# A decoder layer on one core: attention weights split over two tiles, seven products in another order, half-width first batches, separate PSUM tiles for the last rows

## The chip, the core and the metric

The kernel runs on one NeuronCore of a Trainium2 chip. TensorE multiplies matrices (its weight loads are listed apart, as PEld), VectorE (DVE) and ScalarE (ACT) work on SBUF and PSUM, GpSimd (POOL) on SBUF alone, and SyncE (SP) issues most DMAs. Each engine and each DMA queue takes its instructions in order and waits where an operand is not ready. The metric is the device time in microseconds of one execution, median of several.

## The reference, cut to what matters

The input x has 16 batches of 128 rows by 1024, all float32; the context has the same shape. One pre-norm decoder layer is computed:

```python
x = x + attn(layernorm(x))            # one head, d = 256
x = x + xattn(layernorm(x), context)  # 8 heads of 64, linear attention
x = x + ffn(layernorm(x))             # int4 weights, inner width 2752

# attn
q, k, v = split(x @ Wqkv + bqkv)
out = softmax(q @ k.T / 16) @ v @ Wo + bo
# xattn: Wq, Wk, Wv, Wo; softmax of q over a head's channels, of k over the positions
context = k @ v.T ; out = context.T @ q ; out = Wo @ out + bo ; l2-normalised, times g * sqrt(128)
# ffn: weights unpacked from two nibbles a byte, (w - zero) * scale in groups of 64
out = (silu(x @ Wg.T) * (x @ Wu.T)) @ Wd.T
```

## The kernel before, in words

The layer runs in three stages on one core. Self-attention takes about the first 245 us, cross-attention goes on to about 755, and the feed-forward block takes the rest.

*Self-attention* works on four token tiles of 512 tokens, that is four batches each (`TB`, `BPT`, `NT` in the code). Rows are normalised by ScalarE, turned by TensorE transposes through PSUM, and copied into `xnT`, with the 1024 channels on the partitions in eight chunks. In the first tile the opening (`first_rows`) does this batch by batch; its vector instructions are pinned in program order by `InOrder`, a wrapper that asks the planner to keep their order. Then `query_key` multiplies query and key blocks f = 0 to 3 directly, each in two halves of 256 tokens. In the three later tiles `query_key_products` computes all of query and key by a Strassen-like scheme: seven products of quarter-size operands instead of eight. The operands on the weight side are quarters of the query and key weights and their sums S1, S2, S4 (`weight_sums`); on the data side they are quarters of `xnT` and their sums T1, T2, T3, made by VectorE. Products 1, 6, 5 and 3 add up in one PSUM bank, read by ScalarE or VectorE between them; products 7 and 4 share another; product 2 has its own.

Beside a tile's products stand pieces of other work. `beside(f)` adds the output bias on GpSimd, takes statistics of a coming batch, gives a finished batch of the tile before its output projection (`give`, L330 and L337), and turns a batch of the next tile. `value(i)` multiplies a value block. `next(early)` runs one step of `prepare`, which unpacks the feed-forward weights: SP loads packed bytes (`raw`) and scales (`sz`), VectorE unpacks into `pa` and combines into `pc`, GpSimd stores them to DRAM. These vector steps are pinned among themselves. Where nothing is pinned, a planner orders each engine's instructions by program order and by its own estimates of when operands are ready; it also orders the SP queue.

*Memory.* Pools are stacked from the left and from the right of SBUF. Self-attention's pool `a_w` holds the joint weight tile `wqkv_sb` (24 KB a partition: queries and keys in the first 16, values in the last 8), then the output weights, biases and S1, S2, S4. When self-attention is over, the pools of cross-attention take the same left place (`unit_pool`), in the order `b_ek`, `b_as`, `b_cx`, `b_0`, `b_w`, `b_3`; with `reuse_waits="tile"` a new tile waits for the last users of the old tiles that lie where it comes to lie. So the two context tiles `cx` (`load_ctx`, L790) lie 16 KB up, on the values' part of the joint tile, and `wk_sb`, `wq_sb` (L805, L811) on biases. The context's transpose `cxt` and `wo_again`, a second copy of the output weights for the last four batches, lie on the right.

*Cross-attention* starts with four key units of its first batch (`key_unit`: context chunk by `wk_sb`, then an exponential on ScalarE into `ek`, then a product with `cxt`). From line 692 on TensorE, VectorE and SP instructions are pinned, so whatever stands first in these streams holds up the rest.

*The last product.* The down projection is a scheme of seven outer products with seven inner ones each, in the orders `DOWN` and `INNER`. The last inner product (2) of the last outer one (4) ends the kernel: it adds to the PSUM tile of product 1, four batches wide, first for rows 0 and 1, then for rows 2 and 3; `got` adds the kept sum `U` for each row and sends it out.

## Time and profile before

| What | Value |
|---|---|
| Median of three runs | 2178.35 us (2177.74 to 2178.78) |
| Profiled execution, its own time | 2177.33 us |
| Its span in the profile | 2175.5 us |
| Mean granted TensorE clock | 0.997 |
| TensorE busy | 2147.1 us, 99% of the span |
| Weight loads busy | 1671.9 us, 77% |
| VectorE busy | 1547.0 us, 71% |
| DMA, mean over the span | 218 GB/s |

Durations and stretches are read from the profiled execution; 1.8 us of its time lie outside its span. In a row of the timeline the first number is the start in us from the span's start, the second the length in us, then engine, line, operation, output and inputs, shapes, and the number of instructions taken together; a bracket gives the engine's idle time before it and what ended that. A matmul of float32 appears as two instructions. In the list of waits a row gives who waited for whom, the total in us, how often, and the longest. TensorE instructions of one row overlap in the array, so their number divided into the length gives their spacing, and that is shorter than the duration of one.

### The profile page before, as it was taken

How to read it: one execution, taken by the hardware profiler on the slowest of the kernel's cores; microseconds unless marked ns; L12 is line 12 of the kernel's file. 1: busy time of each engine (PE TensorE's matmuls, PEld its weight loads, DVE VectorE, ACT ScalarE, POOL GpSimd, SP SyncE). 2: the span in 40 equal slices, each digit the busy share in tenths (PEclk: the TensorE clock that was granted, in tenths of full speed). 3: DMA queues.
4: the chain of work that ended last, by engine and by line, in shares of the span. 5: the costliest groups of instructions: out<-in, count | busy, mean ns of one | idle time of the engine just before them, and what ended most of it. 6: DMA issues, size and time to landing. Idle time of an engine off the chain costs nothing.

```text
span 2175.5 us, 26039 instructions
## 1 busy us (share of the span) xinstructions
PE 2147.1 (99%) x9148; PEld 1671.9 (77%) x9148; DVE 1547.0 (71%) x2102; ACT 546.7 (25%) x746; POOL 796.7 (37%) x675
## 2 busy tenths in 40 slices
PE   8999899999999999999999999999999999999998
PEld 7877545555555558888888888888886788888887
DVE  5989678888888758786777987878774445534573
ACT  4121135555655551212111212112111000000000
POOL 5343224333433345544444554444441022333200
PEclk9999999999999999999999999999999999999999
DMA  6445537777787576877888746677667578979941
GB/s 259 131 149 187 187 126 236 226 228 236 236 267 245 184 235 216 291 254 257 268 291 278 241 141 215 205 228 244 207 207 232 186 201 241 282 197 258 269 124 60
DMA packets 272205, 474.59 MB, mean 218 GB/s; under 512 B 29633, under 2 KB 128321, under 8 KB 266177
## 3 DMA queue, kind: packets, MB, share of 16 engines
q1 hardware_dynamic: 226736, 383.02, 54.6%
q0 software_dynamic: 27456, 71.45, 12.1%
q10 hardware_dynamic: 17872, 18.36, 2.6%
q8 instruction: 75, 1.23, 0.2%
q14 instruction: 66, 0.53, 0.1%
HBM read 314.64 MB, written 157.55 MB: 217 GB/s over the span
## 4 chain that ended last, share of the span: by engine, by line
PE 93%; DVE 4%; issue 1%; DMA 1%; ACT 0%; SPq 0%; POOL 0%; DVEq 0%; ACTq 0%; POOLq 0%
PE q L80 38%; PE po L2031 22%; PE kq L80 10%; PE mm L80 8%; PE kx L80 5%; PE p L80 3%; PE mm L451 2%; PE mm L436 1%; DVE pa L80 1%; PE mm L573 1%; PE mm L330 1%; DMA cx<-in_cx 1%; DVE pc L80 0%; PE tr L381 0%; DVE bnst L147 0%
## 5 line engine op out<-in xcount | busy, mean ns | idle before, releaser
L80 PE MATMUL q<-ti,li 128*128 128x256 f32 x1680 | 385.4, 379 | 0.0
L80 PEld LDWEIGHTS q<-ti,li 128*128 128x128 f32 x1680 | 319.2, 190 | 43.4
L80 ACT COPY k<-q 128x512 f32<-128x512 f32 x210 | 123.1, 586 | 661.1 <-PE q L80 642.6
L80 POOL TENSOR_TENSOR li<-w 128x512 f32<-128x512 f32 x140 | 203.3, 1458 | 52.0 <-PE q L80 34.5
L974 POOL TENSOR_TENSOR qe<-qe,qrec 128x1024 f32<-128x1024 f32 x64 | 146.3, 2286 | 175.2 <-DVE qrec L80 156.6
L80 POOL TENSOR_TENSOR li<-w,li 128x512 f32<-128x512 f32 x70 | 107.8, 1541 | 259.4 <-PE q L80 239.4
L2031 PE MATMUL po<-wc,lc 128*128 128x256 f32 x840 | 183.4, 379 | 0.0
L2031 PEld LDWEIGHTS po<-wc,lc 128*128 128x128 f32 x840 | 159.6, 190 | 21.8
L80 DVE TENSOR_TENSOR C<-q,k 128x512 f32<-128x512 f32 x150 | 102.8, 685 | 71.8 <-PE q L80 67.4
L80 PE MATMUL q<-b,w 128*128 128x256 f32 x640 | 151.2, 379 | 0.0
L80 POOL TENSOR_TENSOR li<-li,w 128x512 f32<-128x512 f32 x70 | 91.4, 1306 | 123.1 <-PE q L80 122.8
L80 PEld LDWEIGHTS q<-b,w 128*128 128x128 f32 x640 | 121.6, 190 | 17.0 <-issue 0.5
L80 PE MATMUL q<-ti,w 128*128 128x256 f32 x560 | 132.3, 379 | 0.0
L80 PE MATMUL kq<-wk_sb,cx 128*128 128x512 f32 x256 | 121.9, 599 | 7.8 <-DMA cx<-in_cx 7.8
L80 PEld LDWEIGHTS mm<-qs,m_sb 128*128 128x128 f32 x512 | 97.3, 190 | 40.1 <-issue 29.9
L2031 PE MATMUL po<-wq,lq 128*128 128x256 f32 x560 | 126.8, 379 | 0.8 <-DVE m L80 0.8
L80 PE MATMUL kx<-ek,cxt 128*128 128x512 f32 x256 | 121.7, 598 | 0.0
L80 DVE STREAM_TRANSPOSE kt<-qe 128x1024 f32<-128x1024 f32 x64 | 79.2, 1238 | 58.9 <-POOL qe L974 56.8
L80 PE MATMUL mm<-qs,m_sb 128*128 128x256 f32 x512 | 120.8, 379 | 0.0
L80 PE MATMUL kq<-wq_sb,xn 128*128 128x512 f32 x256 | 120.2, 593 | 0.4 <-ACT qe L962 0.4
L2031 PEld LDWEIGHTS po<-wq,lq 128*128 128x128 f32 x560 | 105.9, 190 | 16.7 <-DVE m L80 1.2
L80 PEld LDWEIGHTS q<-ti,w 128*128 128x128 f32 x560 | 106.4, 190 | 14.5
(220 smaller groups left out, 3751.0 us busy)
## 6 DMA issues: line engine op xcount, KB each, us to landing
ti<-r SPq DMA_DIRECT2D x36, 1024.0 KB, 7.6
w<-wg SPq DMA_DIRECT2D x140, 256.0 KB, 3.2
w<-wu SPq DMA_DIRECT2D x140, 256.0 KB, 3.9
lq<-h SPq DMA_DIRECT2D x140, 256.0 KB, 5.2
kd<-kt SPq DMA_DIRECT2D x62, 512.0 KB, 3.5
qs<-kd SPq DMA_DIRECT2D x244, 128.0 KB, 3.1
h<-h SPq DMA_DIRECT2D x80, 256.0 KB, 3.1
wq<-wd SPq DMA_DIRECT2D x70, 256.0 KB, 7.0
```

What stands on the lines that cost most here:

```text
L80: return lambda *args, **kw: self._tc.keep_in_program_order(fn(*args, **kw))
L330: tensor.matmul(ps, oT[:, d, ts(b % BPT, S)], wo_d[d][:, ts(h, 512)], start=(d == 0), stop=(d == 1),)
L436: nc.tensor.matmul(ps[:, tokens], wqkv_sb[:, f, c, :], xnT[:, c, tokens], start=(c == 0), stop=(c == CC - 1),)
L451: nc.tensor.matmul(ps, xnT[:, c, ts(i, S)], wqkv_sb[:, 4:6, c, :], start=(c == 0), stop=(c == CC - 1),)
L573: nc.tensor.matmul(ps[:, n], L[p][:, n, c], R[p][:, c], start=(p == first and n == c == 0), stop=(p in (2, 3, 4) and c == HC - 1), skip_gr ...
L974: nc.gpsimd.tensor_tensor(qe, qe, rec.unsqueeze(2).to_broadcast(wide), ALU.mult)
L2031: nc.tensor.matmul(bank[:, i, :], l[:, ts(i, S)], w,  start=(start and c == 0 and i % 2 == 0), stop=(stop and c == len(pairs) - 1), skip_g ...
```

## The change

The diff has four parts.

1. The opening. Batches 0 and 1 are normalised in two halves of 512 columns, each in its own tile. `first_rows` becomes a generator: it returns before batches 2 and 3 are turned, and these two are turned after the first and the second query block. The statistics of batches 4 to 7 are pinned on VectorE and stand behind it.
2. The products. TensorE's product matmuls are pinned. Their order goes from 1, 7, 6, 2, 5, 4, 3 to 1, 2, 7, 6, 5, 4, 3, the first value block stands between 5 and 4, and the steps of weight preparation are placed one by one (`steps(n)`). In the last token tile the value block that came before the products now comes after product 6, one `give` stands between 5 and 4, and 5 instead of 8 preparation steps come before product 3 in program order, with one left over after the loop.
3. The memory. A pool `a_q` below `a_w` holds the query and key weights (16 KB) and S1, S2, S4; the value weights get their own tile `wv_sb` in `a_w`. Among cross-attention's pools `b_cx` and `b_w` come first, so that context tiles and `wk_sb`, `wq_sb` lie on the query and key weights; `b_0` comes to lie on the value weights.
4. The end. The last inner product keeps rows 0 and 1 in product 1's PSUM tile and puts rows 2 and 3 into tiles of their own (of products 6 and 5). What product 1 holds for rows 2 and 3 is added to `U` by VectorE earlier, at inner product 5.

```diff
+        tc.tile_pool(name="a_q", bufs=1) as aq,
         tc.tile_pool(name="a_w", bufs=1) as aw,
...
-        wqkv_sb = aw.tile([P, 6, CC, P], F32, name="wqkv_sb")
+        wqk_sb = aq.tile([P, 4, CC, P], F32, name="wqk_sb")
+        wv_sb = aw.tile([P, 2, CC, P], F32, name="wv_sb")
...
+            normed = {}
+
             def rows(b):
-                xn = a2.tile([P, C], F32, name="xn")
                 row_shift(b, vector)
-                normalise_act(xn, X[b], b)
-                halves[b] = turn_half(xn, xnT, b, 0)
-                nc.scalar.copy(*turn_half(xn, xnT, b, 1))
+                xn = normed[b] = [
+                    a2.tile([P, C], F32, name="xn") for _ in range(2 if b < 2 else 1)
+                ]
+                n = C // len(xn)
+                for h, t in enumerate(xn):
+                    normalise_act(t[:, ts(h, n)], X[b][:, ts(h, n)], b)
+
+            def turn_rows(b):
+                halves[b] = turn_half(normed[b][0], xnT, b, 0)
+                nc.scalar.copy(*turn_half(normed[b][-1], xnT, b, 1))
...
-            for b in range(1, BPT):
-                half(b, 0)
-                rows(b - 1)
-                if b > 1:
-                    copy(b - 2)
-                half(b, 1)
-            rows(BPT - 1)
-            copy(BPT - 2)
-            copy(BPT - 1)
+            half(1, 0)
+            rows(0)
+            turn_rows(0)
+            half(1, 1)
+            half(2, 0)
+            rows(1)
+            turn_rows(1)
+            copy(0)
+            half(2, 1)
+            copy(1)
+            half(3, 0)
+            rows(2)
+            half(3, 1)
+            rows(3)
+            yield
+            turn_rows(2)
+            copy(2)
+            yield
+            turn_rows(3)
+            copy(3)
...
-        S1, S2, S4 = (aw.tile([P, 2, HC, P], F32, name=f"S{n}") for n in (1, 2, 4))
+        S1, S2, S4 = (aq.tile([P, 2, HC, P], F32, name=f"S{n}") for n in (1, 2, 4))
...
-                        nc.tensor.matmul(
+                        tensor.matmul(
...
+            if t == 0:
+                for f in range(4):
+                    halves[f] = aps.tile([P, TB], F32, name="mm")
+                    query_key(f, xnT, qkT, halves[f], ts(0, HALF))
+                    next(opening, None)
+                for b in range(BPT, 2 * BPT):
+                    row_stats(b, InOrder(tc, nc.vector))
...
-                for i in (2, 3) if more else ():
-                    value(i, xnT, v)
+                if more:
+                    value(2, xnT, v)
+                    value(3, xnT, v)
                 third()
-                value(0, xnT, v)
-                for f, ps in enumerate(((1, 7), (6, 2), (5, 4), (3,))):
-                    for p in ps:
-                        product(p)
-                    if f < 2 or not more:
-                        beside(f)
-                    elif f == 2:
-                        next(early)
-                value(1, xnT, v)
-                at = weigh(qkT)
+                for p in (1, 2, 7):
+                    product(p)
+                beside(0)
+                steps(3)
+                product(6)
+                beside(1)
+                steps(2)
+                if not more:
+                    value(0, xnT, v)
+                product(5)
                 if more:
+                    value(0, xnT, v)
+                else:
+                    give((t - 1) * BPT, oT)
+                product(4)
+                if more:
+                    steps(1)
+                    product(3)
+                    value(1, xnT, v)
+                    at = weigh(qkT)
                     beside(2)
+                    steps(2)
                     turned = []
                     beside(3, lambda: turned.append(turn_weights(at)))
+                    steps(2)
                     atT = turned.pop()
                 else:
-                    for i in range(1, BPT):
+                    beside(2)
+                    beside(3)
+                    product(3)
+                    value(1, xnT, v)
+                    at = weigh(qkT)
+                    steps(1)
+                    for i in range(2, BPT):
+                        value(i, xnT, v)
                         give((t - 1) * BPT + i - 1, oT)
-                        if i > 1:
-                            value(i, xnT, v)
-                        next(early, None)
+                        steps(2)
...
+    bcx = unit_pool("b_cx", 2)
+    bw = unit_pool("b_w", 1)
     bek = unit_pool("b_ek", 3)
     bas = unit_pool("b_as", 1)
-    bcx = unit_pool("b_cx", 2)
     b0 = unit_pool("b_0", 2)
-    bw = unit_pool("b_w", 1)
...
-                            start=(start and c == 0 and i % 2 == 0),
+                            start=(start and c == 0 and (i % 2 == 0 or len(rows) == 1)),
...
-                    for rows in (range(2), range(2, BPT)):
-                        multiply(ps, pairs, False, True, rows)
-                        got(oq, (0, 0), ps, only=rows)
+                    multiply(ps, pairs, False, True, range(2))
+                    got(oq, (0, 0), ps, only=range(2))
+                    for i, q in ((2, 6), (3, 5)):
+                        own = dps[q].tile(wide, F32, name=f"po{q}")
+                        multiply(own, pairs, True, True, (i,))
+                        got(oq, (0, 0), own, only=(i,))
...
+                    if oq == DOWN[-1]:
+                        apart = U[0, 0][:, 2:]
+                        vector.tensor_tensor(apart, bank[1][:, 2:], apart, ALU.add)
```

## The prediction

> **What bounds the kernel now.** I read the busy table first, then the list of who waited for whom, then the busy time by stage, then the three places where TensorE waits. The busy table:
>
> ```profile
> PE 2147.1 (99%) x9148; PEld 1671.9 (77%) x9148; DVE 1547.0 (71%) x2102; ACT 546.7 (25%) x746; POOL 796.7 (37%) x675
> ```
>
> TensorE is idle for 2175.5 - 2147.1 = 28.4 us of the span, and the change takes away no matmul. So what can be won lies in those 28.4 us and in instructions that run slower than their kind. The waits of TensorE:
>
> ```profile
> PE tr L381 <- ACT xn L164: 8.2, 1, 8.2
> PE kq L80 <- DMA cx<-in_cx: 7.8, 1, 7.8
> PE mm L573 <- DVE qkT L561: 2.7, 2, 1.7
> PE mm L573 <- ACT qkT L555: 0.9, 1, 0.9
> PE po L2031 <- DVE m L80: 0.8, 1, 0.8
> ```
>
> The reader sees one wait for each part of the change: 8.2 at the start, 7.8 at the crossing from self-attention to cross-attention, 2.7 + 0.9 in the seven products, 0.8 at the last tile. By stage (stretch, its length, then busy time of PE, PEld, DVE, ACT, POOL, granted clock, DMA share, GB/s):
>
> ```profile
> 145.00:188.00 43.00, 41.27 (x195) 31.03 (x195) 38.88 (x59) 11.05 (x26) 16.95 (x23) 1.00 0.44 147
> 188.00:245.00 57.00, 56.07 (x246) 43.23 (x244) 56.69 (x91) 6.83 (x20) 21.29 (x37) 1.00 0.63 207
> ...
> 245.00:250.00 5.00, 0.24 (x3) 0.05 (x1) 2.27 (x6) 0.59 (x1) 1.50 (x3) 0.96 1.02 405
> 250.00:253.00 3.00, 0.00 (x0) 0.01 (x1) 0.00 (x0) 0.00 (x0) 0.00 (x0) 0.50 1.05 389
> 253.00:255.00 2.00, 1.98 (x3) 0.97 (x4) 0.00 (x0) 0.00 (x0) 0.00 (x0) 0.50 0.49 127
> ```
>
> From 188 to 245 VectorE is busy 56.69 of 57 us, most of it weight preparation (tiles pa, pc): beside TensorE it is the second bound there, and a term won on TensorE in this stage is only kept where VectorE's part comes in time. From 245.24 to 253.02 TensorE has nothing, the DMA engines are full (405 GB/s), and the granted clock falls to 0.50. The crossing in order of time:
>
> ```profile
> 235.97 3.62 PE L451 MATMUL mm<-wqkv_sb,xnT 128*128 128x256 f32 x16
> ...
> 239.66 0.33 SPq L810 DMA_DIRECT2D wo_again<-in_wo  x1
> ...
> 241.81 0.46 SPq L790 DMA_DIRECT2D cx<-in_cx  x1
> ...
> 253.02 5.35 PE L80 MATMUL kq<-wk_sb,cx 128*128 128x512 f32 x8 [7.78 <-DMA cx<-in_cx]
> ...
> 255.66 0.15 DVE L80 TENSOR_SCALAR gs_sb<-gs_sb 128x1 f32<-128x1 f32 x1 [8.32 <-DMA gs_sb<-in_xg]
> ```
>
> The last value product ends at 239.4, SP starts issuing at 239.66, the context load goes out fifth at 241.81 and lands 11.1 us later. The whole queue of attention loads is 0.25 us behind that last read of the joint weight tile. The start and the end:
>
> ```profile
> 8.20 3.83 PE L381 MATMUL tr<-ident,xn 128*128 128x128 f32 x16 [8.20 <-ACT xn L164]
> ...
> 12.55 2.07 PE L436 MATMUL mm<-xnT,wqkv_sb 128*128 128x256 f32 x4 [0.52 <-DVE xnT L80]
> ...
> 18.53 15.71 PE L436 MATMUL mm<-xnT,wqkv_sb 128*128 128x256 f32 x72
> ```
>
> ```profile
> 2163.73 2.42 PE L2031 MATMUL po<-wq,lq 128*128 128x256 f32 x10 [0.85 <-DVE m L80]
> ...
> 2169.22 0.76 DVE L80 TENSOR_TENSOR m<-po,u 128x256 f32<-128x256 f32 x2 [5.54 <-PE po L2031]
> ```
>
> **Part 1, the opening.** Removed: the order in which TensorE meets the transposes of batches 2 and 3 before query block 0 is done (only 8 of its 16 instructions run before 18.53). Added: two half activations for batches 0 and 1 in place of one. The trace has no such half from SBUF here; the 128x512 activation of qkT takes 0.69, the full one 1.24. So the first transposes start at 6.91 + 0.69 = 7.6 instead of 8.20. Batch 1's first half is ready at 8.77 + 0.69 = 9.46, its four transposes at 0.21 each end at 10.3, its copy on VectorE no longer stands behind a bn_stats (0.68) and a shift (0.16) and runs at 10.5 to 11.2. The query weights are there: the first block was issued at 2.60 and its load takes about 7.8, so 10.4; the other three land at about 11.6, 12.9 and 14.3. Block 0 starts at 11.2 instead of 12.55.
>
> From there stand 64 instructions of the four first halves and 16 transposes without a wait. Before, the first halves ended at 18.53 + 56 x 15.71/72 = 30.75. What I don't know is the rate: before, instructions ran at half rate from 8.20 to about 17.5 (0.427 apart in the row at 12.55, 0.218 in the row at 18.53), for 9.3 us, although the granted clock is listed as 1.00. With half rate until 7.6 + 9.3 = 16.9: 13.3 instructions by then, 50.7 x 0.218 + 16 x 0.11 = 12.8 after, end 29.7, gain 1.0. With full rate from 11.2: end 26.9, gain 3.8. Against this: VectorE's statistics of batches 4 to 7 now stand in order behind the copy of batch 3, which comes after block 1 on TensorE, about 22.8. Copy 0.7, four statistics at 1.45, rstd 0.2, POOL 1.0, shift 0.2 and one activation of 1.25 end at 32; TensorE wants that batch's transposes at 34.24 less the gain. So the cover is about 1 us and vanishes with a larger gain. I take **-1.2**, near the row of half rate, with ends +0.5 (the statistics come later than worked out) and -3.8.
>
> The Trainium skill ("TensorE: Matmul & The Clock Gate", section "Part 1: The HAM clock gate (the "warmup" mystery)") has the array go to full rate after one busy window of some 3.4 us. Counted from 11.2 this would be 14.6, an estimate from that page, with the first halves done at 28.5 and a gain of 2.2; the case's own stretch of 9.3 us with small holes of 0.52 speaks for less, and the sum goes by the row.
>
> **Part 2, the products.** No instruction is added. Products 2 and 7 change places with 6, the first value block goes between 5 and 4, and the preparation steps move. In the second and third token tile product 3 waited 1.02 and 1.73 for the vector add of product 5, because only product 4 (3.45) lay between. Now a value block (3.45) and product 4 lie between, 6.9 us, so both waits go: -2.75. What they need keeps its place: 7 comes 13.8 us after the tile's start before and after, 6 comes 21.6 after it in both, and 4 comes 11.2 after 6 in both. In the last tile the 0.93 wait of 6 for an ACT read goes too, since 2 and 7 now stand between 1 and 6. But there value block 0 no longer comes first: 7 is wanted 6.9 us after the tile's start (188.0), at 194.9, and its operand T3 was written at 196.61 to 197.83, behind preparation steps. Pinned, TensorE can't take another product meanwhile: +2.9. Sum -2.75 - 0.93 + 2.9 = **-0.8**; ends -3.7 (T3 in time) and +3.0 (VectorE, saturated, is later by what TensorE has gained, and nothing of the first two waits is kept). Three of 36 preparation steps move behind the last weighing; VectorE does the same total, and after 247.33 it had 8.3 us free.
>
> **Part 3, the crossing.** Query and key weights get a tile at the bottom of the stack, and the context tiles and wk, wq lie on it. Its last readers are products 4 and 3, over by 216.98 before and by about 219 in the new order, at least 20 us ahead of 241.81. Loads of 256 or 512 KB took 3.3 to 11.2 us here, so even the longest is over. Removed: the wait of 7.78, and the half rate after it (8 instructions in 5.35 against 8 x 0.43 = 3.43: 1.92). Together -9.70. What is late next: the key product needs PSUM banks read by the last vector add (ends 245.71) and ACT copy (245.28 + 0.59 = 245.87), 0.6 behind the last matmul. Further on, left at their old times, cxt (landed 247.2, first used 258.21) allows 11.0 us, wvo (255.2, used 266.88) 11.6, the second context (257.6, used 272.06) 14.4. The closest is VectorE: its in-order stream opens with gs_sb at 255.66, whose load stood behind xbo_sb, which waited until 253.0 for the last stores of prepared weights. From there ones, shift, one X add (0.69) and the key sum (1.21) free the first ek buffer at 257.9, and ACT used it again at 266.99: 9.1 us allowed. Those stores landed in the full stretch; 1 MB less in it (context, wk, wq) is 2.5 us at 405 GB/s, so some 11.5 allowed, against 1.2 + 0.8 + 9.7 = 11.7. I take off 0.6 for the banks and 0.6 for this: **-8.5**; ends -9.7 and 0 (the loads still go out behind wo_again).
>
> **Part 4, the end.** Rows 2 and 3 get own banks: TensorE no longer waits 0.85 for the vector read of rows 0 and 1. After the last matmul one add remains (0.43) of two (0.76). Added: one vector add of 128x512, 0.69 as its kind, about 30 us earlier; VectorE has 3.23 us idle right behind it. **-1.2**; ends -0.8 and -1.3.
>
> **Parts costed at nothing.** The reordered pools put feed-forward's fourth weight tile on wq, read until 751.5; it is first used near 798, and before the change these loads went out only at 756.69, so some 40 us cover a load of 4.4. Its cost if SP issues it early and holds the qs loads behind it: up to 3 us. Between 255 and 2160 all else shifts as it is.
>
> **Sum:** -1.2 - 0.8 - 8.5 - 1.2 = -11.7. The profiled execution took 2177.33 (span 2175.5 and 1.8 around it), 1.0 below the median of 2178.35: 2165.6 + 1.0 = **2166.6**.
>
> **Rivals.** *A, the first loads do not go early:* SP is one queue in order, its order set by the planner's own estimates, and before the change wo_again went out ahead of wk and cx. If it still does, it waits for the last value block at 239.4, and parts 1, 2 and 4 alone remain, 3.2: 2175.1, down to 2172 if the fuller stretch shortens by 2.5. Against it: wk and cx come first in program order and are now free 20 us sooner. *B, every term at its good end:* 3.8 + 3.7 + 9.7 + 1.3 = 18.5, 2160; against it stands that VectorE is busy 56.69 of 57 us and does not get faster. *C, slower: the pinned products wait for VectorE in the last tile.* T1, T2 and T3 there queue behind preparation steps of 2.5 to 3.3 us each. Before, TensorE filled the time with other products. The stall is 2.9 at the old lag of 9.8 us and grows 1:1; from a lag of 9.8 + 11.7 = 21.5 us, four to five more steps ahead of T3, it eats everything and the time is 2178 or more; with six, about 2183. For it: VectorE's saturation and the pinning. Against it: as many steps (25) precede that tile as before.
>
> **How the numbers follow.** Forecast 0.66, A 0.16, B 0.08, C 0.10. The forecast's own range, with part 3 between -6 and -9.7 and the others about half way to their ends, is 2161.5 to 2172. The range for 8 in 10 takes in most of B and about the middle of A: 2160.5 to 2175.5. A difference of 0.2% (4.4 us) is what a measurement of this kernel tells from none: 2174.0 to 2182.7. Forecast, B and half of A are faster: 0.82; half of A and a fifth of C are within: 0.10; the rest of C slower: 0.08.
>
> **What would show it.** Right: the list of waits without cx, and cx issued before 230; key products 0.43 apart from the first; product 3 without a wait in tiles two and three; the first 64 query instructions over before 30; no wait on m at the end and a single add after the last matmul. Wrong: a new wait on T3 (product 7, last tile) above 3 us, on gs_sb or ek behind the crossing, on xn near 32, or SP holding cx behind wo_again.

## The result, and the profile after

The changed kernel takes 2182.32 us (median; 2181.16 to 2183.83), the kernel before in the same runs 2177.66 us (2174.9 to 2179.53). The ratio is 1.0024 with a 95% interval of 1.0015 to 1.0033: slower by 4.7 us, where 11.7 us less were forecast, and above the forecast range of 2160.5 to 2175.5. The profiled execution took 2182.9 us, with a span of 2181.1 against 2175.5.

The busy table after, and below it the list of TensorE's waits (who waited for whom: total, times, longest):

```profile
PE 2150.2 (99%) x9148; PEld 1673.9 (77%) x9148; DVE 1556.1 (71%) x2103; ACT 547.0 (25%) x748; POOL 799.6 (37%) x675
```

```profile
PE tr L383 <- ACT xn L164: 10.6, 3, 7.6
PE kx L80 <- DMA cxt<-in_cxt: 7.5, 1, 7.5
PE mm L80 <- DVE xnT L586: 4.1, 1, 4.1
PE mm L80 <- DVE qkT L583: 1.0, 2, 0.7
```

Each part did what its text says. The wait on `cx` (7.8) is gone, the waits of product 3 on qkT shrank from 2.7 to 1.0, the wait on `m` at the end is gone. But three waits took their places: 2.8 us more on `xn` in the opening, 4.1 on T3 (`xnT`, product 7 of the last tile), 7.5 on `cxt`. TensorE idles 2181.1 - 2150.2 = 30.9 us instead of 28.4, and its busy time is 3.1 longer for the same number of instructions, because some ran at half rate.

Where the difference arises, by the starts of the same rows in the two profiles:

| Row | before | after | difference |
|---|---|---|---|
| opening done (two value blocks after the weighing) | 53.18 | 55.50 | +2.3 |
| last tile starts (value block 0 before, product 1 after) | 188.0 | 188.56 | +0.6 |
| key product of cross-attention starts | 253.02 | 251.30 | -1.7 |
| product `wvo`, 14 to 22 us on | 266.88 | 273.24 | +6.4 |
| feed-forward starts (`p`) | 755.08 | 761.43 | +6.4 |
| last vector add ends | 2169.98 | 2175.00 | +5.0 |

The opening loses 2.3 here, and the kernel before has a late one: in the other profiles with the old opening the first of these rows stands at 51.07 to 52.61. The second and third tile win 1.7. The last tile loses: it takes 62.7 from its first matmul to the key product, while before TensorE had run out of work 57.2 after it. The key product is early and that is worth nothing, because the next one waits. The end wins 1.4; 0.6 more passes between the last add and the end of the span.

*The opening.* The timeline of the kernel after (start, length, engine, line, operation; in brackets the idle time before and what ended it):

```profile
27.85 2.35 POOL L450 TENSOR_TENSOR X<-X,bo_sb 128x1024 f32<-128x1024 f32 x1 [14.01 <-DMA bo_sb<-in_bo]
30.17 1.03 POOL L153 TENSOR_TENSOR rstd<-rstd,mhalf 128x4 f32<-128x4 f32 x1
31.16 13.97 POOL L450 TENSOR_TENSOR X<-X,bo_sb 128x1024 f32<-128x1024 f32 x6
31.23 2.30 DVE L159 SCALAR_TENSOR_TENSOR shift<-mv,rstd 128x4 f32<-128x4 f32 x1 [3.37 <-POOL rstd L153]
34.90 1.97 PE L383 MATMUL tr<-ident,xn 128*128 128x128 f32 x8 [2.79 <-ACT xn L164]
36.66 4.23 PE L457 MATMUL mm<-xnT,wqk_sb 128*128 128x256 f32 x16
```

The first halves of query and key end 2.2 earlier, as the section on the prediction works out. But the statistics of batches 4 to 7 are late, and when GpSimd's reciprocal root is due, a bias addition stands ahead of it: 2.35 us. The shift, an operation on four elements in a row, then takes 2.30 us instead of 0.16, exactly as long as GpSimd's next addition lasts. So `xn` comes 2.79 after TensorE wanted it, and after that wait the transposes run at half rate (1.97 for eight instead of 1.04) and the next 16 matmuls still take 4.23 instead of 3.62.

*The crossing.* The timeline of the kernel after:

```profile
199.70 6.39 PE L80 MATMUL mm<-xnT,wqk_sb 128*128 128x256 f32 x16 [4.08 <-DVE xnT L586]
...
230.29 0.42 DVE L479 TENSOR_TENSOR v<-mm,bv_sb 128x256 f32<-128x256 f32 x1 [5.78 <-PE mm L472]
...
235.40 0.76 DVE L80 TENSOR_SCALAR pa<-raw 128x512 int32<-128x512 int32 x2
...
251.30 3.65 PE L80 MATMUL kq<-wk_sb,cx 128*128 128x512 f32 x8
...
257.20 1.22 DVE L80 TENSOR_TENSOR pa<-pa,sz 128x1024 f32<-128x1024 f32 x1
258.45 0.82 SPq L833 DMA_DIRECT2D cxt<-in_cxt  x2
...
262.42 3.75 PE L80 MATMUL kx<-ek,cxt 128*128 128x512 f32 x4 [7.47 <-DMA cxt<-in_cxt]
```

The same two steps in the timeline of the kernel before:

```profile
239.24 1.21 DVE L80 TENSOR_TENSOR pa<-pa,sz 128x1024 f32<-128x1024 f32 x1
240.48 0.33 SPq L792 DMA_DIRECT2D cxt<-in_cxt  x1
```

In both kernels `cxt` goes out 0.03 us after the last preparation step has multiplied `pa` by `sz` (239.24 + 1.21 = 240.45; 257.20 + 1.22 = 258.42). That step is 18.0 us later in the kernel after. Two rows of busy time by stage (stretch, length, then PE, PEld, DVE, ACT, POOL, clock, DMA share, GB/s), before and then after, show that VectorE had room meanwhile:

```profile
225.00:250.00 25.00, 20.24 (x78) 12.97 (x76) 22.27 (x44) 2.35 (x7) 9.06 (x16) 0.99 0.57 206
```

```profile
225.00:250.00 25.00, 25.00 (x106) 17.77 (x105) 16.40 (x29) 3.14 (x12) 4.76 (x9) 1.00 0.53 178
```

After, VectorE is idle for 8.6 of these 25 us while preparation remains to be done. It waits 5.78 for a value block, and more for the weighing: its queue runs in order, and the remaining steps stand behind the weighing in it.

### The profile page after: what moved, and what is told of

Its sections match the earlier page's. It is cut to its first block, busy times and chain, and to the rows that moved or that the text cites. A ratio compares the mean times of both kernels' runs of the same rounds, so it can differ in the third digit from the quotient of the medians.

```text
span 2181.1 us, 26039 instructions
## 1 busy us (share of the span) xinstructions
PE 2150.2 (99%) x9148; PEld 1673.9 (77%) x9148; DVE 1556.1 (71%) x2103; ACT 547.0 (25%) x748; POOL 799.6 (37%) x675
## 3 DMA queue, kind: packets, MB, share of 16 engines
q8 instruction: 75, 1.23, 0.2%
## 4 chain that ended last, share of the span: by engine, by line
PE 92%; DVE 4%; DMA 1%; issue 1%; ACT 1%; POOL 0%; SPq 0%; DVEq 0%; POOLq 0%; ACTq 0%
PE q L80 38%; PE po L2072 22%; PE mm L80 10%; PE kq L80 10%; PE kx L80 5%; PE p L80 3%; PE mm L472 2%; DVE pa L80 2%; PE mm L330 1%; DMA bo_sb<-in_bo 1%; DVE pc L80 1%; PE mm L457 1%; DVE bnst L147 0%; DMA wqk_sb<-in_wqkv 0%; DVE C L80 0%
```

## The experiments

All times are medians. The kernel before took 2176.8 to 2177.2 us beside them, and the ratios are to it. "After" means the changed kernel, 2182.32; beside it the kernel before took 2177.66, so a difference to after may be 0.4 to 0.9 too large.

### Each part alone

Part 3 alone: the kernel before with the separate tiles for query and key weights and the new order of cross-attention's pools.

```diff
+        tc.tile_pool(name="a_q", bufs=1) as aq,
-        wqkv_sb = aw.tile([P, 6, CC, P], F32, name="wqkv_sb")
+        wqk_sb = aq.tile([P, 4, CC, P], F32, name="wqk_sb")
+        wv_sb = aw.tile([P, 2, CC, P], F32, name="wv_sb")
...
+    bcx = unit_pool("b_cx", 2)
+    bw = unit_pool("b_w", 1)
     bek = unit_pool("b_ek", 3)
```

> The kernel before with part 3 alone: the two weight tiles and the reordered pools; opening, products, steps and end as before. Theory (the places are good, the steps behind the last weighing spoilt them): cx is issued before 230, the wait of 7.78 and the half rate behind it go but for about 1 us, 7.5 to 9.7 us: 2168 to 2170 against 2177.7. Rival (the places do not help, another load of the same queue takes cx's part): a wait of 5 us or more on cxt or wo_again, 2175 to 2179.

Measured 2167.15 us, ratio 0.9958 (0.9944 to 0.9971): 10.0 us won. The timeline of this kernel at the crossing:

```profile
214.69 1.24 SPq L792 DMA_DIRECT2D cx<-in_cx  x1
239.55 0.33 SPq L794 DMA_DIRECT2D cxt<-in_cxt  x1
244.14 3.65 PE L80 MATMUL kq<-wk_sb,cx 128*128 128x512 f32 x8
247.62 1.88 PE L80 MATMUL kx<-ek,cxt 128*128 128x512 f32 x4
```

`cxt` goes out at its old time, neither key product waits, and nothing runs at half rate. The part is good, and the kernel after has lost it.

Part 2 alone: the kernel before with the product loop of the diff in place of its own.

```diff
-                for f, ps in enumerate(((1, 7), (6, 2), (5, 4), (3,))):
...
+                for p in (1, 2, 7):
+                    product(p)
+                beside(0)
+                steps(3)
...
```

> The kernel before with part 2 alone: product order, pinning, value block and preparation steps of the changed kernel, but the old opening, memory places and end. Theory (what part 2 wins in the second and third tile, about 1.9, is lost in the last tile by T3 and the cold array, 5.5, and the moved steps keep the crossing as late as before or later by up to 2): 2180.5 to 2184. Rival (the steps matter only together with the new places): the crossing wait stays at 7.8 or below and the time is 2178 to 2180.

Measured 2179.83 us, ratio 1.0011 (1.0002 to 1.0020): 2.6 us lost. TensorE waits 4.1 for T3, and at the crossing 2.0 that the profile puts down to a preparation step (`pa`), and 5.1 for `cxt`. The 7.8 for `cx` is gone without part 3: TensorE comes 2.1 later (247.34 against 245.24), and `cx`, issued at 241.74 as before, takes 7.5 to 8.1 to land instead of 11.1. By that `cx` lands near 249.2, when the wait of 2.0 ends (249.39), so either can have ended it.

Part 4 alone: own PSUM tiles for the last two rows.

```diff
-                    for rows in (range(2), range(2, BPT)):
...
+                    for i, q in ((2, 6), (3, 5)):
+                        own = dps[q].tile(wide, F32, name=f"po{q}")
+                        multiply(own, pairs, True, True, (i,))
...
```

> The kernel before with part 4 alone. Forecast: the wait of 0.85 us on m goes and one add of 0.33 behind the last matmul: 1.2 us, 2176.5 against 2177.7. Rival (the store of the last row comes no earlier, or the added vector add delays inner product 6 or 7): no change.

Measured 2176.01 us, ratio 0.9994 (0.9985 to 1.0003). The wait on `m` is gone and one add follows the last matmul. The median moves by 1.2, as forecast, but the interval holds no change.

Part 1 undone: the kernel after with the old opening.

```diff
-        opening = first_rows(xnTs[0])
-        next(opening)
+        first_rows(xnTs[0])
...
+                for b in range(BPT, 2 * BPT) if t == 0 else ():
+                    row_stats(b)
```

> The changed kernel with the opening of the kernel before (part 1 undone). Theory (the opening cost 2.4 us net: the third tile of self-attention starts 2.3 later than before although the first query halves end 2.2 earlier): 2179 to 2180.5, the waits on T3 (4.1) and cxt (7.5) unchanged. Rival (the delay is covered by later waits on VectorE): 2181.5 to 2183.

Measured 2177.39 us, ratio 1.0003 (0.9994 to 1.0012), 4.9 below after. So the new opening costs about 4.9 where it was to win 1.2. The waits on T3 (4.1) and `cxt` (7.3) stay.

The sum of the four is -10.0 + 2.6 - 1.2 + 4.9 = -3.7, and the kernel after is at +4.7. The parts lose some 8.4 to one another. The next runs say where.

### Mending one thing at a time

Three preparation steps go back ahead of product 3 of the last tile; the rest of after stands. Eight then stand ahead of the last weighing, as in the kernel before. There, by its code, six of the eight came before product 3 and two behind it, ahead of the weighing; it is the weighing that counts here.

```diff
                     beside(3)
+                    steps(3)
                     product(3)
                     value(1, xnT, v)
                     at = weigh(qkT)
-                    steps(1)
                     for i in range(2, BPT):
                         value(i, xnT, v)
                         give((t - 1) * BPT + i - 1, oT)
-                        steps(2)
+                        steps(1)
```

> The changed kernel, but in the last token tile three of the five preparation steps that stand behind the last weighing stand before product 3, as many as in the kernel before. Theory (VectorE's in-order queue idles 5.8 us for the last values and holds these steps back, the last of them frees the place of cxt): VectorE is busy between 224 and 230, cxt is issued some 8 to 12 us earlier than 258.45, the wait of 7.47 on it and the half rate behind it (4 instructions in 3.75 instead of 1.72) go: 7 to 9.5 us, 2173 to 2175. Rival (the new memory places or the order of SP's queue keep cxt late): cxt is issued after 255 and the time is 2180 to 2183.

Measured 2173.43 us, ratio 0.9985 (0.9976 to 0.9994), 8.9 below after. The timeline of this kernel:

```profile
247.86 3.65 PE L80 MATMUL kq<-wk_sb,cx 128*128 128x512 f32 x8
248.44 0.82 SPq L833 DMA_DIRECT2D cxt<-in_cxt  x2
252.25 1.95 PE L80 MATMUL kx<-ek,cxt 128*128 128x512 f32 x4 [0.74 <-DMA cxt<-in_cxt]
```

`cxt` goes out 10.0 earlier and the wait of 7.47 is 0.74; VectorE is busy 22.23 of the 25 us from 225 on, not 16.40. By the rows, 6.7 come from the wait and 2.1 from the half rate behind it (3.75 and 2.19 for the two groups of four, now 1.95 and 1.88). These 8.9 us are about the 8.4 that the parts lost to one another: part 2 undid most of what part 3 won.

That run moves steps and `cxt` together. The next leaves the steps late and exchanges the places of `cxt` and its neighbours (pool `b_qs`, where `wo_again` lies) on the right of the memory. `wo_again`, not `cxt`, then lies on the tiles `raw` and `sz` that the preparation still reads.

```diff
-    bct = side_pool("b_ct", 2)
...
+    bct = side_pool("b_ct", 2)
```

> The kernel after with the places of cxt and of the two smaller tiles beside it exchanged, so that cxt no longer lies on the raw weights and their scaled copies that the preparation still multiplies; the three preparation steps stay late. Theory: the wait of 7.5 us of kx on cxt came from that place alone: cxt is issued before 245, kx follows kq without a wait over 1 us, the wait moves to the tile that now lies there (issued near 258) and is at most 4 us: 2177 to 2180. Rival: cxt's issue waits for something else (the queue's order, the transfer itself): the wait of kx stays above 6 us and the time at 2181 to 2183.

Measured 2177.86 us, ratio 1.0002 (0.9993 to 1.0011), 4.5 below after. The timeline of this kernel:

```profile
242.75 1.03 SPq L833 DMA_DIRECT2D cxt<-in_cxt  x2
...
246.22 12.38 SPq L851 DMA_DIRECT2D wo_again<-in_wo  x2
...
254.60 1.88 PE L80 MATMUL kx<-ek,cxt 128*128 128x512 f32 x4
...
262.00 1.13 PE L80 MATMUL mm<-wo_again,oT 128*128 128x512 f32 x2 [2.95 <-DMA wo_again<-in_wo]
```

`kx` follows without a wait, and `wo_again`, whose issue now lasts from 246.22 to 258.60, is waited for instead. So `cxt` waited for the place alone, not for its transfer or the queue, and a late preparation is paid by whatever lies on its buffers.

In the last tile, value block 0 goes back ahead of the products, so that T3 has 3.45 us more.

```diff
+                if not more:
+                    value(0, xnT, v)
                 for p in (1, 2, 7):
                     product(p)
...
-                if not more:
-                    value(0, xnT, v)
                 product(5)
```

> The changed kernel, but in the last token tile value block 0 stands before product 1 again, as in the kernel before; the products keep their new order. Theory (product 7 comes too early for T3): the wait of 4.08 on T3 shrinks to 0.6 to 1.0, since 3.45 us of work come before it, and the half rate behind it (16 instructions in 6.39 instead of 3.46) goes: 5.5 to 6.5 us, 2176 to 2177. Rival (VectorE is the bound of this stage, and what TensorE gains here it loses at a later wait on VectorE before 250): the wait moves to another tile of this stage and the time stays at 2181 to 2183.

Measured 2176.15 us, ratio 0.9998 (0.9989 to 1.0007), 6.2 below after. The timeline of this kernel at product 7:

```profile
199.58 3.69 PE L80 MATMUL mm<-xnT,wqk_sb 128*128 128x256 f32 x16 [0.71 <-DVE xnT L586]
```

The wait falls from 4.08 to 0.71, and the 16 instructions take 3.69 instead of 6.39: 3.4 and 2.7, together 6.1 of the 6.2. `cxt` still costs 7.3.

In the opening, the reciprocal roots of batches 4 to 7 and the first four bias additions are pinned on GpSimd, roots first.

```diff
-            nc.gpsimd.tensor_tensor(X[b], X[b], bo_sb, ALU.add)
+            engine = InOrder(tc, nc.gpsimd) if b < BPT else nc.gpsimd
+            engine.tensor_tensor(X[b], X[b], bo_sb, ALU.add)
...
-                row_rstd((t + 1) * BPT, BPT)
+                row_rstd((t + 1) * BPT, BPT, gpsimd=InOrder(tc, nc.gpsimd) if t == 0 else nc.gpsimd)
```

> The changed kernel with one thing more: on GpSimd the rstd of batches 4 to 7 and the bias additions of the first tile are pinned in program order, so that rstd stands ahead of the first bias addition, which waits for the load of bo_sb. Theory (GpSimd's queue made the opening lose): the wait of 2.79 us on xn near 34.9 and the half rate behind it (transposes 1.97 instead of 0.87, the next 16 query instructions 4.02 instead of 3.46, together 1.7) go; up to 4.4 us, 2178 to 2180 against 2182.3. Rival (the statistics pinned behind the copy of batch 3 are too late by themselves): the wait stays above 2 us and the time at 2181.5 to 2183.

Measured 2177.68 us, ratio 1.0006 (0.9997 to 1.0015), 4.6 below after. The timeline of this kernel:

```profile
28.63 1.02 POOL L80 TENSOR_TENSOR rstd<-rstd,mhalf 128x4 f32<-128x4 f32 x1 [14.64 <-DVE rstd L152]
29.61 9.35 POOL L80 TENSOR_TENSOR X<-X,bo_sb 128x1024 f32<-128x1024 f32 x4
29.68 2.30 DVE L159 SCALAR_TENSOR_TENSOR shift<-mv,rstd 128x4 f32<-128x4 f32 x1 [1.13 <-POOL rstd L80]
31.90 1.27 DVE L147 BATCH_NORM_STATS2 bnst<-X 128x6 f32<-128x512 f32 x2
...
33.36 1.09 PE L383 MATMUL tr<-ident,xn 128*128 128x128 f32 x8 [0.56 <-ACT xn L164]
```

The root no longer waits, the wait on `xn` falls from 2.79 to 0.56, and the transposes keep full rate. The 4.6 us are about the 4.9 that the old opening gave back, so the order on GpSimd, with the wait and the half rate that follow, accounts for the loss of the opening. (The profiled execution took 2180.97, 3.3 above the median; its row behind the weighing stands at 52.86, after's at 55.50.) The shift still takes 2.30, because the additions start 0.07 before it.

### All mends, and what each part is then worth

After with the three edits above together:

```diff
+            engine = InOrder(tc, nc.gpsimd) if b < BPT else nc.gpsimd
...
+                if not more:
+                    value(0, xnT, v)
                 for p in (1, 2, 7):
...
+                    steps(3)
                     product(3)
```

> The changed kernel with three things mended together: rstd ahead of the bias additions on GpSimd, value block 0 first in the last tile, three preparation steps back before product 3. Singly they gave 4.6, 6.2 and 8.9 us. Theory (three separate in-order queues): they nearly add up, 2162.5 to 2166; what is lost is lost to VectorE, which does not get faster, as a wait on cxt of at most 4 us. Rival (VectorE is the bound from 145 on, so that the gains overlap): 2168 to 2173, with a wait on cxt or in the last tile that takes them back.

Measured 2164.47 us (2164.12 to 2165.05), ratio 0.9943 (0.9930 to 0.9957). That is 17.9 below after, against a sum of 8.9 + 6.2 + 4.6 = 19.7 for the three alone, and 12.8 below the kernel before. With the three costs gone the kernel is where the forecast (2166.6) saw it, and a little below. That the sum comes out does not mean that its terms do, as the next runs show.

Parts 3 and 4 alone, on the kernel before:

```diff
+        wqk_sb = aq.tile([P, 4, CC, P], F32, name="wqk_sb")
...
+                        own = dps[q].tile(wide, F32, name=f"po{q}")
```

> The kernel before with the moves of the memory's first loads (part 3) and the split of the last PSUM tiles (part 4). Theory: the two gains don't touch each other and add: part 3 alone gave 2167.15 us, part 4 took the wait of 0.85 on m and one 0.42 add from the tail, so 2165.5 to 2166.5. Rival: the tail's gain is lost to something behind it (part 4 alone gave a ratio of 0.9994, an interval that holds 1): 2167 or more.

Measured 2166.0 us (2164.54 to 2167.19), ratio 0.9948 (0.9935 to 0.9962). That is 11.2 won, where the forecast had 9.7 for these two parts and 2.0 for the others. Most of what there is to win needs neither the opening nor the products.

Parts 3 and 4 and the new product order in tiles 2 and 3 alone:

```diff
+                    tensor = nc.tensor
+                    for f, ps in enumerate(((1, 7), (6, 2), (5, 4), (3,))):
+                        for p in ps:
+                            product(p)
+                        beside(f)
+                        steps(2)
```

> The kernel before with parts 3 and 4 and the new order of the products in tiles 2 and 3 alone; the last tile keeps its old loop, with the steps of the preparation among the products. Theory: the order in tiles 2 and 3 gains 1 to 2 us by the shorter waits on qkT and nothing in the last tile is lost: 2163.5 to 2165. Rival: the order of the products is worth nothing anywhere: 2166 or more, as the run with parts 3 and 4 alone.

Measured 2167.29 us (2164.8 to 2168.71), ratio 0.9951 (0.9938 to 0.9965). The gain of 1 to 2 us was not there. In the two profiles the waits on qkT fall from 2.8 to 1.0, but the last tile then waits 1.1 for T3 and the key product 0.7 for `oT`. T3 itself starts later, at 195.53 instead of 194.51: VectorE is full there, and what TensorE wins it waits for later. From the start of the second tile to that of the last it wins 1.8; its opening was 1.5 later in this profile, and from there to the key product it loses 2.1.

The old opening with the mended last tile:

```diff
+        first_rows(xnTs[0])
...
+                    value(0, xnT, v)
...
+                    steps(3)
```

> The kernel after with the old opening (part 1 undone), value(0) ahead of the seventh product in the last tile, and the three preparation steps back ahead of the third product. Theory: an opening whose additions wait their turn on GpSimd and the old opening are worth the same within 1 us, so this gives 2163 to 2165.5, beside 2164.47 with the mended opening. Rival: halved first batches are worth 2 us or more once the additions are out of the way: 2166.5 or more.

Measured 2164.23 us (2164.2 to 2165.33), ratio 0.9942 (0.9928 to 0.9955): equal to the kernel with all three mends and the new opening. So even a mended new opening shows no gain. The reason may lie where both wait. First the timeline of the kernel with three mends, then that of this one:

```profile
45.77 2.34 POOL L451 TENSOR_TENSOR X<-X,bo_sb 128x1024 f32<-128x1024 f32 x1
45.83 2.30 DVE L159 SCALAR_TENSOR_TENSOR shift<-mv,rstd 128x4 f32<-128x4 f32 x1 [9.07 <-POOL rstd L153]
50.08 1.83 PE L488 MATMUL mm<-qkT 128*128 128x128 f32 x14 [1.69 <-ACT qkT L467]
```

```profile
43.32 4.66 POOL L431 TENSOR_TENSOR X<-X,bo_sb 128x1024 f32<-128x1024 f32 x2
43.38 4.63 DVE L159 SCALAR_TENSOR_TENSOR shift<-mv,rstd 128x4 f32<-128x4 f32 x1 [7.36 <-POOL rstd L153]
49.96 1.83 PE L468 MATMUL mm<-qkT 128*128 128x128 f32 x14 [0.26 <-ACT qkT L447]
```

In both, the shift of batches 8 to 11 ends when GpSimd's additions do, near 48.1. On ScalarE `xn` waits for the shift and `qkT`, which the weighing needs, stands behind `xn`. The new opening reaches the weighing 1.3 earlier (48.01 against 49.31) and waits 1.4 longer.

To see whether that event takes the gain, the reciprocal roots of batches 8 to 11 were pinned ahead of the additions for batches 4 to 7, once with each opening. (The old opening had no pins on GpSimd, so it gets those of the first tile as well.)

```diff
-            engine = InOrder(tc, nc.gpsimd) if b < BPT else nc.gpsimd
+            engine = InOrder(tc, nc.gpsimd) if b < 2 * BPT else nc.gpsimd
...
-                row_rstd((t + 1) * BPT, BPT, gpsimd=InOrder(tc, nc.gpsimd) if t == 0 else nc.gpsimd)
+                row_rstd((t + 1) * BPT, BPT, gpsimd=InOrder(tc, nc.gpsimd) if t <= 1 else nc.gpsimd)
```

> The kernel with the three mends (2164.47 us), and besides the reciprocal roots of batches 8 to 11 pinned on GpSimd ahead of the additions for batches 4 to 7. Theory: the weighing no longer waits 1.69 us for qkT near 50 us, the shift of batches 8 to 11 is done before 43, the value x32 row starts at 50.1 to 50.4 instead of 51.74, and the time is 2162.5 to 2163.5. Rival: the gain of the opening ends elsewhere: the row moves by less than 0.5 and the time stays at 2164 to 2165.

Measured 2172.27 us (2171.03 to 2175.0), ratio 0.9979 (0.9970 to 0.9988).

> The same two pins on GpSimd in the kernel with the old opening (2164.23 us). Theory: its wait for qkT near 50 us was only 0.26, so it has that to gain: 2163.8 to 2164.8, and the new opening with the pins is 1 to 2 us below it. Rival: it gains as much as the new opening, and the two stay equal.

Measured 2174.08 us (2172.77 to 2174.82), ratio 0.9987 (0.9978 to 0.9996). Both times miss what was expected by 9 to 10 us, to the slow side, and the pins did not do what they were meant to. The shift of batches 8 to 11 was to be done before 43; pinned, its root goes out at 74.46 instead of 44.78, and in the kernel with four mends the shift follows at

```profile
76.18 2.31 DVE L159 SCALAR_TENSOR_TENSOR shift<-mv,rstd 128x4 f32<-128x4 f32 x1 [0.93 <-POOL rstd L80]
```

The wait at the weighing is gone all the same, in both kernels, because no `xn` of these batches stands ahead of `qkT` on ScalarE any more (with four mends it runs at 78.53). The weighing starts at 49.42 with the new opening and at 50.76 with the old one, and the medians differ by 1.8 us. That fits the reading that this wait hid the opening's gain and doesn't prove it: the two ranges overlap, the array leaves half rate at different times in profiles of one and the same opening (see the end of the next section), and the row behind the weighing, expected at 50.1 to 50.4, came at 51.20.

What cost 8 to 10 us is a second lesson. With three mends six additions follow those of the first tile, between 37.83 and 54.55. Here the pinned ones of batches 4 to 7 stand behind the late root, at 76.13, 94.67, 113.58 and 133.24. From 90 to 110 VectorE is busy all the time, with three mends and with four, and TensorE waits for it. The timeline of the kernel with four mends:

```profile
94.28 3.85 DVE L610 TENSOR_TENSOR T<-xnT,T 128x1024 f32<-128x1024 f32 x1
94.67 2.37 POOL L80 TENSOR_TENSOR X<-X,bo_sb 128x1024 f32<-128x1024 f32 x1
...
108.83 5.17 PE L80 MATMUL mm<-xnT,S 128*128 128x256 f32 x16 [4.83 <-DVE qkT L584]
```

and the same operation in the kernel with three mends:

```profile
93.39 1.21 DVE L610 TENSOR_TENSOR T<-xnT,T 128x1024 f32<-128x1024 f32 x1
```

The last three additions fell among VectorE's operations there, and each lengthened the one that it met to between 3.26 and 3.85 us instead of 1.21. That is 2.0 to 2.6 us each and 7.1 together (2.64 + 2.39 + 2.05), for a time that rose by 7.8. On TensorE it arrives as the wait of 4.83 (0.72 with three mends) with half rate behind it (5.17 for 16 matmuls instead of 3.72), and as a wait of 2.01 for T3 in the third tile.

## Why the prediction was wrong, step by step

**The step that failed** is the last sentence of part 2: "Three of 36 preparation steps move behind the last weighing; VectorE does the same total, and after 247.33 it had 8.3 us free." It counted VectorE's work and not its order. The total was the same, but steps behind the weighing can't begin before TensorE has weighed, and VectorE idled 8.6 us of 25 ahead of them. The part was right about the number of steps and costed their delay at nothing; the delay is 8.9 us. More was lost beside it, in the wait on T3 and in the opening, as follows.

**Part 3** was right by itself: -8.5 forecast, -10.0 measured alone, just past its good end of -9.7; loads early, key products 0.43 apart, no wait for banks or `ek`. Its check for what is late next had the right row and read it wrongly: "left at their old times, cxt (landed 247.2, first used 258.21) allows 11.0 us". `cxt` does not keep its time. Its issue follows the last step of the preparation, and the profile of before showed this: 240.45 and 240.48. That step moved by 18.0, 7.0 more than the allowance of 11.0. That the wait is so near to it, 7.47, is luck: the load landed in 3.8 instead of 6.7, and TensorE wanted it 3.3 earlier (254.95 against 258.21). To see that a wait was coming, it was enough to ask what `cxt` itself had waited for.

**Part 2**, apart from the steps: the waits of product 3 were to go, -2.75, and 1.0 of them stayed. The wait on T3 was forecast at 2.9 and is 4.08. Left out was the half rate behind it, 2.77 more (6.39 against 3.62). The prediction had the price of half rate in part 3 (1.92 for 8 instructions) and did not use it here. Its own end of +3.0 was exceeded: by these rows the part comes to -1.75 - 0.93 + 4.08 + 2.77 = +4.2 even without the steps, and with value block 0 first the kernel is 6.2 faster.

**Part 1.** Near: the first transposes start at 7.60 (forecast 7.6, by luck: the half activation takes up to 0.81, not 0.69, and began 0.17 earlier), the first block at 11.87 (11.2). The first halves end at 28.5 (the row of 48 instructions from 21.58, the first 32 of them at 0.216), not at 29.7, so 2.2 are won there, not 1.0. The array left half rate sooner than the 9.3 us taken from the profile of before: 16 instructions in 4.51 us are 5 at 0.427 and 11 at 0.216, so at about 14.0. The Trainium skill's estimate in the prediction ("TensorE: Matmul & The Clock Gate", section "Part 1: The HAM clock gate (the "warmup" mystery)") was 14.6 and 28.5, and was the nearer one in this profile. That confirms neither figure: worked out in the same way, the same opening left half rate at about 11.8 in the kernel with three mends (3.53 us for the first 16 instructions from 11.60) and at about 15.3 in that with the pins on GpSimd (5.15 from 11.92).

Wrong: "So the cover is about 1 us and vanishes with a larger gain." The danger was seen and even listed (a wait on `xn` near 32), but the chain left out GpSimd's additions. The statistics were done at 27.65; a root of 1.02, a shift of 0.16 and an `xn` of 1.25 would have ended near 30.5, ahead of the 32.11 at which TensorE wanted it. An addition of 2.35 went ahead of the root, and the shift took 2.30. That costs about 4.9 with the half rate, beyond the end of +0.5.

**Part 4** was right: no wait on `m`, one add behind the last matmul, -1.2 in the median, too small to be told from nothing by itself.

**The rivals.** A and B did not come. C, given 0.10, named the right mechanism for a third of the loss: product 7 waits for T3. It put its price down to preparation steps ahead of T3 and to a lag of 21.5 us. The wait came at a smaller lag (T3 was ready 11.1 after the tile's start), and the larger loss was behind it, in preparation steps that were too late for the memory and not in the way of a product. The chance of 0.08 for a slower kernel was too small: three costs, each with a row that bore on it, were taken at too little or at nothing together. (By the forecast's fixed limit of 2182.7 the median of 2182.32 would still count as no difference; beside the kernel before in the same runs it is slower.)

What stays open: with parts 3 and 4 in place, the four kernels between 2164.2 and 2167.3 differ by about as much as one kernel's runs do, so the order of the products in tiles 2 and 3 and the old loop of the last tile can't be told apart by 1 us. The opening adds to that. The same old opening starts the transposes of batch 4 at 34.08 in the profile of before and at 31.97 in that of parts 3 and 4 alone. In the first its eight transposes at 14.42 take 1.91, at half rate; in the second those at 13.29 take 1.04. When the array leaves half rate there differs from run to run by some 2 us, and with the new opening by up to 3.5 (11.8 to 15.3, above); no run here sets it.

The wait on `xn` in the unmended new opening differs too: 2.79 in the profile of after, 2.32 and 2.26 in those with value block 0 first and with `cxt` moved, and 1.79, with no half rate behind it, in that with the steps early, whose row behind the weighing stands at 53.04 instead of 55.50. So the opening's cost of 4 to 5 us rests on the medians, not on one profile.

## What to carry to other kernels

When a transfer is left "at its old time", look up what its issue waited for. If it lies on buffers of other work, that work's last step is its due time, and moving the step moves the transfer. Equal work on an engine that runs in order is not equal time: a step put behind something that waits for TensorE waits as well, though the engine has room before. A wait of more than about 2 us that a change adds on TensorE is to be priced with the half rate that followed such waits here.

## What the runs showed of the hardware

- A VectorE operation that reads two tensors of SBUF stood still while GpSimd added 128x1024 in SBUF: the shift of 128x4 took 0.16 alone and 2.30 or 4.63 beside one or two additions, a 128x1024 operation 1.21 alone and up to 3.85. `BATCH_NORM_STATS2`, which reads one, took 1.23 to 1.27 in the middle of the additions, as alone. A `TENSOR_SCALAR` of 128x4 with one input was held as well (up to 1.97, alone 0.17). The page "SBUF — State Buffer" of the Trainium skill (section "SBUF: two separate sides") has it so: a port shared by VectorE and GpSimd is held for a whole instruction, and VectorE needs it with two SBUF inputs or in a 2-port mode; which mode the one-input operations ran in, no run here shows. The page gives the port to whichever instruction starts first. The recorded starts don't show that: three of the lengthened 128x1024 operations of the kernel with four mends (at 94.28, 102.20, 113.44) begin 0.39, 0.21 and 0.14 before the addition that holds them up, and when an instruction asks for the port the trace doesn't tell. The profile of before showed it too (a shift of 2.32 at 41.96), off the path.
- TensorE waits of up to 2.05 us (1.30, 1.39, 1.69, 1.79, 2.05) left it at full rate. After waits from 2.26 on (2.26, 2.32, 2.79, 4.08, 4.83, 5.13, 7.47) instructions ran at half rate; after one of 2.95 the first two (1.13) did not, and the four behind them did (3.46 instead of 1.88). The prices: 1.93 for eight transposes instead of 1.04 after 2.26, 5.39 to 6.68 for 16 matmuls instead of 3.62 after 4.07 or 4.08, 3.75 for four of 128x512 instead of 1.88 after 7.47.
